# Neighbour lists of a four-layer graph network: the lists of 18 of 26 tiles made inside the first layer, in four parts, instead of all lists ahead of it

## The chip, the cores and the metric

The kernel runs on one core of a Trainium2 chip. A core has a matrix engine (TensorE, PE in the profile), a vector engine (VectorE, DVE), a scalar engine (ScalarE, ACT), a general engine (GpSimd, POOL) and an engine that mainly starts transfers (SyncE, SP). Each runs its own queue of instructions in order; they wait for one another through semaphores. The metric is the device time of one execution in microseconds (us). The kernel before takes 2420.07 us, the median of three runs (2419.6 to 2422.44).

## The reference

There are 3327 nodes with 512 features each, and a 0/1 matrix `adj` of 3327 x 3327 with about 0.5% ones, symmetric and with a full diagonal. Four graph-attention layers follow one another, each of this kind:

```python
h = jnp.maximum(_layernorm(x, axis=-1), 0.0)
h = (h @ W).reshape(n, heads, d)
e = leaky_relu(e_src[:, None, :] + e_dst[None, :, :])   # e_src, e_dst: h times two vectors
e = jnp.where(mask[:, :, None], e, -jnp.inf)            # mask: the neighbours in adj
alpha = jax.nn.softmax(e, axis=1)
x = x + jnp.einsum('ijh,jhd->ihd', alpha, h)
```

The layers have 8, 4, 1 and 8 heads; some of them end with an ELU. The sorted tiles are dimensioned for at most 11 to 36 neighbours, so a layer needs, for every node, the rows of its few neighbours and not the whole matrix.

## The kernel before, in words

**The first stage** (functions within `tile_gat_stack`) reads `adj` in 26 tiles of 128 rows. For each row it finds the columns of the neighbours, up to 40 of them, and keeps them in `L` (128 x 26 x 40, line 633). It also projects the features of the first layer and writes them as rows into the table `tabx` in device memory. Nodes are then sorted by their number of neighbours: `rank` (line 742) is a node's place in that order, `hi` the tile of 128 places it falls into and `lo` its place within the tile (lines 747 to 750). Tile 0 holds the nodes with most neighbours (36 at most), tile 25 those with fewest (11 at most); `CAPS` has these bounds.

**The lists.** The loop at line 764 carries each node's neighbours from the node's first place to its sorted place. It is a product with one-hot matrices: `low[:, t, :]` (line 781) is 1 where a column is the `lo` of the node in that row; the right side (`every`, line 774, or `spare`, line 785) has the neighbour numbers of tile t's nodes in the columns of the tile named by `hi`, and zeros elsewhere; 26 matmuls (line 789) add up one part. There are two parts: part a, the tiles 18 to 25 (120 columns), and part b, the tiles 1 to 17 at 25 columns each and tile 0 at 36 (461 columns). ScalarE copies each result into `idx` and, doubled, `twice` (lines 790 and 791). Part b's right sides go through two buffers in turn, so VectorE and TensorE take turns. After this comes the branch of line 793, on a flag `bad`; the normal case goes to `tile_gat_lists`.

**The layers** (`tile_gat_lists`). A layer goes through the sorted tiles from 25 down to 0. A tile's neighbours are taken in groups: in the first layer 3 gathers first, one of them of a double row that also holds the node's own `x`, then 4 at a time. One group is one step of a loop written out by hand; its pieces are put into each engine's queue in the order in which the loop emits them. For a step s:

- `fetch` (line 865): GpSimd starts one gather for each neighbour (line 838, `g<-tabx`), each moving 128 rows named by a column of `idx` or `twice`. The buffers `g` exist five times (`LOOK`), so the gathers of a group need the products of the group five before it to be done.
- `scored` (line 882) of step s + 1: VectorE adds and bends the scores (`z`, lines 900 and 902), ScalarE takes the exponential (line 903). In the first layer ScalarE also replaces the list entries by ranks (line 906) and keeps the node's own row in `x` (line 908).
- `group` (line 912) of step s: VectorE multiplies each neighbour's row by its weight (line 931, `m<-g` or `bank<-g`), and TensorE adds the rows up in a bank (line 936). As scores of step s + 1 stand ahead of the products of step s in VectorE's queue, the products of a group wait for the rows of the next group too.
- When a tile's last group is done, its `divisors`, `means`, `added`, `root` and so on follow over the next steps, then four transposes (line 454) and the projection for the next layer (line 472), whose rows SyncE writes to the table `tab`.

The first layer has more in its steps. `Weights` of the next layer are loaded as soon as the object is made, ahead of the layer (lines 393 and 395), and `fold` (lines 408 and 410) multiplies them by the attention vectors: three folds after each of the steps 0, 1 and 2 (eight in all). For the third layer, which treats its nine largest tiles densely, nine `Mask` steps, at places 18, 28, ..., gather whole rows of `adj` into `low` (1.7 MB each), ScalarE makes them bf16 (line 1050), TensorE transposes them, and ScalarE puts the pieces into a part of `L` (line 1062), from which SyncE writes them to `found`, four pieces for each mask. `low` and `L` are free by then, as the lists are done.

Of the kernel before, what the change touches and what calls it, by code (L numbers as in the profile page):

```python
# [38 lines left out]
ROUND = 1.5 * 2.0 ** 23  # L39

# [340 lines left out]
class Weights:  # L381
# [3 lines left out]
    def __init__(self, nc, pool, work, l, ws, avs):  # L385
        F = ws[l].shape[0]
        HF, KC = F // 2, F // P
        self.l, self.H, self.D = l, HEADS[l], F // HEADS[l]
        self.nc, self.work, self.HF = nc, work, HF
        self.w = pool.tile([P, KC, 2, HF + 8], F32, name="w")  # L390
        self.av = pool.tile([P, 2, F], F32, name="av", bufs=1)
        for s in range(2):
            nc.sync.dma_start(self.w[:, :, s, :HF],
                              ws[l][:, s * HF:(s + 1) * HF].rearrange("(k p) n -> p k n", p=P))
            nc.sync.dma_start(self.av[:, s, :], bass.AP(tensor=avs[l].tensor, offset=avs[l].offset + s * F,
                                                        ap=[[0, P], [1, F]]))
        if self.H < 8:
            nc.vector.memset(self.w[:, :, :, HF + self.H:], 0.0)
        self.left = [(s, k) for s in range(2) for k in range(KC)]

# [98 lines left out]
class Slots:  # L499
# [16 lines left out]
    def __init__(self, pool, NT):  # L516
        self.parts = [self.Part(pool, "a", [(18, NT)]), self.Part(pool, "b", [(1, 18), (0, 1)])]
# [10 lines left out]
def tile_gat_stack(ctx: ExitStack, tc: tile.TileContext, x, adj, adjT, ws, avs, out):  # L528
# [32 lines left out]
    spare = late.tile([P, 2, slots.parts[1].columns], F32, name="spare")  # L561


    with ExitStack() as c1:
# [39 lines left out]
        def constants():  # L604
            nc.gpsimd.memset(ones, 1.0)
            nc.gpsimd.memset(upper, 1.0)
            nc.gpsimd.affine_select(upper, upper, [[1, P]], OP.is_gt, 0.0, base=0, channel_multiplier=-1)
            nc.gpsimd.memset(sofar, 0.0)
            nc.gpsimd.memset(base[:, 0:1], 0.0)
            nc.scalar.activation(ahead, counting(P, 1, 0, 0), AF.Copy)  # L610
            nc.scalar.activation(bins, counting(BINS, -1, KMAX, 0), AF.Copy)
            nc.scalar.activation(one, ones[:, 0:1], AF.Copy)

# [77 lines left out]
        with tc.manual_schedule(engines={mybir.EngineType.Pool, mybir.EngineType.DVE}):  # L691
            for t in range(NT):
# [6 lines left out]
                if t == 1:  # L699
                    W = Weights(nc, wpool, work, 0, ws, avs)  # L700
# [12 lines left out]
                if t == 0:  # L713
                    constants()
# [20 lines left out]
        with tc.manual_schedule(engines={mybir.EngineType.Pool, mybir.EngineType.PE,  # L735
# [10 lines left out]
            hi = small.tile([P, NT], F32, name="hi", bufs=1)  # L746
# [6 lines left out]

            junk = small.tile([P, BINS], F32, name="junk")
# [3 lines left out]
            nc.tensor.matmul(pn[0:1, :3], ones[:, 0:1], wrong, start=True, stop=True)  # L758
            worst = small.tile([1, 1], F32, name="worst", bufs=1)
            nc.vector.tensor_reduce(worst, pn[0:1, :3], AX.X, OP.max)  # L760
            nc.vector.tensor_copy(bad, worst)


            for i, part_ in enumerate(slots.parts):
                t0, t1 = min(b[0] for b in part_.blocks), max(b[1] for b in part_.blocks)
                high = fixed[:, 304:512] if i == 0 else ps_k.tile([P, BANK], F32, name="high")
                high = high[:, :NT * (t1 - t0)].rearrange("p (t h) -> p t h", h=t1 - t0)
                nc.vector.tensor_tensor(high, ahead[:, t0:t1].unsqueeze(1).to_broadcast([P, NT, t1 - t0]),
                                        hi.unsqueeze(2).to_broadcast([P, NT, t1 - t0]), OP.is_equal)
                n = part_.columns  # L770
                if i == 0:
                    (_, _, k, _), = part_.blocks
                    every = once.tile([P, NT, n], F32, name="every")
                    nc.vector.tensor_tensor(every.rearrange("p t (h k) -> p t h k", k=k),
                                            L[:, :, :k].unsqueeze(2).to_broadcast([P, NT, t1 - t0, k]),
                                            high.unsqueeze(3).to_broadcast([P, NT, t1 - t0, k]), OP.mult)
                pi = ps_i.tile([P, BANK], F32, name="pi")
                for t in range(NT):
                    if i == 0:
                        rhs = every[:, t, :]  # L780
                        nc.vector.tensor_scalar(low[:, t, :], ahead, lo[:, t:t + 1], None, OP.is_equal)
                    else:
                        rhs = spare[:, t % 2, :]
                        for b0, b1, k, c in part_.blocks:
                            nc.vector.tensor_tensor(
                                rhs[:, c:c + (b1 - b0) * k].rearrange("p (t k) -> p t k", k=k),
                                L[:, t, :k].unsqueeze(1).to_broadcast([P, b1 - b0, k]),
                                high[:, t, b0 - t0:b1 - t0].unsqueeze(2).to_broadcast([P, b1 - b0, k]), OP.mult)
                    nc.tensor.matmul(pi[:, :n], low[:, t, :], rhs, start=(t == 0), stop=(t == NT - 1))
                nc.scalar.activation(part_.idx, pi[:, :n], AF.Copy)  # L790
                nc.scalar.activation(part_.twice, pi[:, :n], AF.Copy, scale=2.0)
# [3 lines left out]
    with cond.Else():  # L795
        tile_gat_lists(tc, x, adj, ws, avs, out, ident, half, slots, L, low, spare, tabx, tabs)
# [3 lines left out]
def tile_gat_lists(ctx: ExitStack, tc: tile.TileContext, x, adj, ws, avs, out, ident, half, slots, L, low, spare, tabx, tabs):  # L800
# [24 lines left out]
    xs = [xpool.tile([P, F], F32, name=f"x{t}") for t in range(NT)]  # L825
# [8 lines left out]
    nc.vector.memset(zero, 0.0)  # L834
    L, low, spare = [t.rearrange("p a b -> p (a b)") for t in (L, low, spare)]
# [13 lines left out]
    class Tile:  # L849
# [29 lines left out]
        def scored(self, i):  # L879
# [20 lines left out]
            nc.vector.tensor_tensor(z, g[:, :n, ROW - 8:ROW - 8 + H],  # L900
# [133 lines left out]

    class Mask:
# [5 lines left out]
        def fetch(self):  # L1041
            self.a = low.bitcast(I32)
            gather(self.a, adj, slots(self.t, 0))
# [15 lines left out]
        def keep(self, c0, c1):  # L1059
            def piece():  # L1060
                u = L.bitcast(U8)[:, c0 * P:c1 * P]
                nc.scalar.activation(u, self.pt[:, :(c1 - c0) * P], AF.Copy)
                n = P // 4
                nc.sync.dma_start(found.rearrange("(j p) c -> p j c", p=P)[:, c0:c1, self.t * n:(self.t + 1) * n],
                                  u.bitcast(I32).rearrange("p (j c) -> p j c", c=n))
# [299 lines left out]
    for l in range(NL):  # L1365
# [3 lines left out]
        with ExitStack() as c2:  # L1369
# [30 lines left out]
            else:  # L1400
                scores = itertools.cycle([pools["p"].tile([P, BANK], F32, name="pw") for _ in range(2)])
# [4 lines left out]
            if l == 0:  # L1406
                for t in range(ND):
                    steps.insert(18 + 10 * t, (Mask(t), 0))
                steps[-8:] = [s for i, step in enumerate(steps[-8:]) for s in (step, (Ranked(i), 0))]
                steps += [(Ranked(j), 0) for j in range(8, NT)]  # L1410
            if whole:
# [5 lines left out]
            for s in range(-1, at_end):  # L1417
# [16 lines left out]
                if s == 16 and l + 2 < NL:  # L1434
                    following = Weights(nc, wpool, work, l + 2, ws, avs)
                if l == 0 and s in (0, 1, 2):
                    for _ in range(3):
                        W.fold()
# [46 lines left out]
```

## Time and profile before

| what | value |
| --- | --- |
| median of three runs | 2420.07 us |
| profiled execution, its own time | 2419.54 us |
| its span in the profile | 2417.8 us |
| PE, DVE, ACT, POOL busy | 2068.3, 1885.1, 936.3, 1739.5 us |
| sorting done (`lo`), from the span's start | 257.35 us |
| part a of the lists made (`low` of line 781, matmuls, copies) | 257 to 270.8 us |
| part b made | 268.7 to 295.7 us |
| first gather of the first layer issued | 271.24 us |
| first product of the first layer | 300.76 us |
| first layer's gathers end | about 900 us |

How to read it: "busy" is the time in which an engine executed instructions; the time it spends in starting transfers is shown as idle with the remark "issue". A line of a timeline gives start and duration in us, engine, source line, operation, output and inputs, how many were merged, and in brackets the idle time just before and what ended it. A group has its busy time, the mean of one instruction in ns, and its idle time. In the table of windows, each engine has its busy time and, in brackets, its number of instructions; "PEclk" is the clock granted to TensorE as a share of full speed.

### The profile page before, as it was taken

To read this page: it belongs to the slowest core of one execution; us is meant where nothing else is said; L and a number is where in the kernel's file an instruction comes from. 1 tells how busy PE (TensorE), PEld (TensorE's weight loads), DVE (VectorE), ACT (ScalarE), POOL (GpSimd) and SP (SyncE) were. 2 spreads that over 40 slices of the span, in tenths; PEclk is the share of its full clock that TensorE was granted. 3 is DMA by queue.
4 is the path that set the end of the run, shared out by engine and by line. 5 is a ranking of instruction groups with operands and counts; after the bars stand their busy time and mean duration, and the time that the engine had idled before them with its cause. 6 is when DMAs were issued, how large, how long until landed. Compare 5 with 4: busy or idle time off the path is not lost.

```text
span 2417.8 us, 27489 instructions
## 1 busy us (share of the span) xinstructions
PE 2068.3 (86%) x7298; PEld 1197.0 (50%) x7298; DVE 1885.1 (78%) x4857; ACT 936.3 (39%) x2528; POOL 1739.5 (72%) x1717
## 2 busy tenths in 40 slices
PE   2778779888988885898999987899898699999997
PEld 1656334444444432454455544456565465556653
DVE  7988788877777763888888884888878578888886
ACT  5777113434331111433333332544443444344430
POOL 7899267777777776766677772778778467777775
PEclk9988899999999997999999998999999899999999
DMA  5887569999998788887888884889887578888885
GB/s 227 316 299 248 153 192 299 276 299 282 286 283 237 234 231 241 242 245 235 234 261 255 256 237 141 270 262 283 268 248 240 161 226 256 250 243 246 252 241 176
DMA packets 260732, 594.23 MB, mean 246 GB/s; under 512 B 103699, under 2 KB 121107, under 8 KB 256214
## 3 DMA queue, kind: packets, MB, share of 16 engines
q0 software_dynamic: 124368, 432.13, 59.5%
q1 hardware_dynamic: 132454, 153.45, 19.6%
q10 hardware_dynamic: 3744, 6.82, 0.8%
q8 instruction: 59, 0.97, 0.2%
q14 instruction: 107, 0.88, 0.1%
HBM read 542.60 MB, written 49.65 MB: 245 GB/s over the span
## 4 chain that ended last, share of the span: by engine, by line
DVE 31%; DMA 17%; PE 16%; issue 13%; POOL 12%; ACT 9%; DVEq 0%; SPq 0%; ACTq 0%; POOLq 0%
DVE m L931 13%; POOL g L838 8%; DMA g<-tab,idxb 6%; PE bank L936 5%; DMA g<-tabx,twiceb 4%; PE pv L472 4%; PE whole L1173 3%; POOL key L698 3%; DVE bank L924 3%; ACT r L1280 2%; DMA g<-tab,idxa 2%; DVE room L1296 2%; DVE z L902 2%; ACT pw L903 2%; DVE z L900 1%
## 5 line engine op out<-in xcount | busy, mean ns | idle before, releaser
L936 PE MATMUL bank<-m,ident 128*128 128x512 f32 x2414 | 1128.0, 613 | 144.8 <-DVE m L931 144.3
L838 POOL DMA_INDIRECT g<-tab,idxb x712 | 683.1, 959 | 236.0 <-issue 162.0
L931 DVE TENSOR_TENSOR m<-g,pw 128x512 f32<-128x512 f32 x1207 | 752.2, 682 | 100.2 <-ACT pw L903 99.6
L936 PEld LDWEIGHTS bank<-m,ident 128*128 128x128 f32 x2414 | 448.7, 194 | 689.2 <-issue 314.6
L472 PE MATMUL pv<-w,hT 128*128 128x264 f32 x1664 | 431.5, 413 | 67.8 <-ACT hT L461 44.5
L903 ACT ACTIVATE pw<-z 128x32 f32<-128x32 f32 (+4 forms) x356 | 68.2, 191 | 988.9 <-DVE z L902 988.9
L472 PEld LDWEIGHTS pv<-w,hT 128*128 128x128 f32 x1664 | 331.7, 203 | 166.8 <-ACT hT L461 50.8
L838 POOL DMA_INDIRECT g<-tab,idxa x297 | 286.3, 964 | 165.0 <-issue 110.6
L838 POOL DMA_INDIRECT g<-tabx,twiceb x342 | 324.0, 947 | 106.0 <-issue 79.5
L1173 PE MATMUL whole<-ve,em 128*128 128x512 f32 x468 | 217.8, 612 | 16.3 <-DVE em L1152 11.2
L698 POOL TENSOR_TENSOR key<-a,keys 128x3328 int32<-128x3328 int32 (+1 forms) x29 | 189.3, 6530 | 16.3 <-DVE cand L707 11.8
L924 DVE SCALAR_TENSOR_TENSOR bank<-g,L,bank 128x512 f32<-128x512 f32 x243 | 183.3, 754 | 6.8
L900 DVE TENSOR_TENSOR z<-g,pw 128x32 f32<-128x32 f32 (+4 forms) x356 | 62.6, 176 | 152.1 <-DMA g<-tabx,twiceb 64.7
L1314 PEld LDWEIGHTS whole<-L,room 128*128 128x128 f32 x1248 | 147.5, 190 | 24.9 <-issue 19.1
L838 POOL DMA_INDIRECT g<-tabx,twicea x99 | 94.9, 959 | 78.5 <-issue 38.1
L1314 PE MATMUL whole<-L,room 128*128 128x130 f32 x1248 | 147.8, 274 | 0.0
L707 DVE MAX8 cand<-key 128x8 f32<-128x208 int32 x416 | 144.0, 364 | 0.1
L1173 PEld LDWEIGHTS whole<-ve,em 128*128 128x128 f32 x468 | 88.1, 196 | 109.2 <-issue 87.2
L1280 ACT ACTIVATE r<-low,L 128x384 f32<-128x384 f32 x208 | 121.2, 583 | 5.1
L454 PE MATMUL pt<-ident,xn 128*128 128x128 f32 x416 | 65.4, 281 | 35.4 <-ACT hT L461 13.6
L454 PEld LDWEIGHTS pt<-ident,xn 128*128 128x128 f32 x416 | 52.5, 145 | 68.6 <-issue 28.3
L931 DVE TENSOR_TENSOR bank<-g,pw 128x512 f32<-128x512 f32 x74 | 51.5, 696 | 37.4 <-ACT pw L903 36.6
(180 smaller groups left out, 2192.6 us busy)
## 6 DMA issues: line engine op xcount, KB each, us to landing
a<-in_adj SPq DMA_DIRECT2D x25, 1664.0 KB
tab<-v SPq DMA_DIRECT2D x78, 264.0 KB
ve<-tab SPq DMA_DIRECT2D x78, 264.0 KB
g<-tab SPq DMA_DIRECT2D x65, 264.0 KB
tabx<-vx SPq DMA_DIRECT2D x26, 528.0 KB
g<-tab,idxb POOLq DMA_INDIRECT x712, 4.0
low<-tab SPq DMA_DIRECT2D x52, 132.0 KB
spare<-tab SPq DMA_DIRECT2D x52, 132.0 KB
```

What stands on the lines that cost most here:

```text
L454: nc.tensor.transpose(pt[:, k, :], xn[:, k * P:(k + 1) * P], ident)
L472: nc.tensor.matmul(pv[:, s, :HF + 8], hT[:, k, :], W.w[:, k, s, :], start=(k == 0), stop=(k == KC - 1))
L698: nc.gpsimd.tensor_tensor(key[:, c:c + quarter], a[:, c:c + quarter], keys[:, c:c + quarter], OP.mult)
L707: nc.vector.max(cand[:, g * 8:(g + 1) * 8], key[:, g * SEG:(g + 1) * SEG])
L838: nc.gpsimd.indirect_dma_start(out=out_, out_offset=None, in_=table, in_offset=bass.IndirectOffsetOnAxis(ap=which, axis=0))
L903: nc.scalar.activation(self.wt[:, k0:k0 + n, :H], z, AF.Exp)
L924: nc.vector.scalar_tensor_tensor(acc, v, w, acc, OP.mult, OP.add)
L931: nc.vector.tensor_tensor(out_.rearrange("p (s h d) -> p s h d", s=2, d=D), v.rearrange("p s (h d) -> p s h d", d=D), wt[:, k0 + q, :H].re ...
L936: nc.tensor.matmul(self.po, ident, m[:, q, :], start=False, stop=(k0 + q == K - 1), skip_group_check=True)
L1173: nc.tensor.matmul(tl.po.rearrange("p (s m) -> p s m", s=2), e[:, q * P:(q + 1) * P], v.rearrange("p (s m) -> p s m", s=2)[:, :, :F // 2], ...
L1280: nc.scalar.activation(self.r[:, h, :], self.a[:, g, :], AF.Relu, bias=-1.0, scale=self.b[:, j, g:g + 1])
L1314: nc.tensor.matmul(dst, e[:, h, q * P:(q + 1) * P], mov, start=False, stop=(j == NT - 1), skip_group_check=True)
```

## The change

The list `slots` has five parts instead of two: a with the tiles 18 to 25 as before (120 columns), b with 14 to 17 (68 columns), c with 9 to 13 (95), d with 4 to 8 (105) and e with 1 to 3 and 0 (111). Only part a is made ahead of the branch, together with nine columns `own` for the nodes' own places in tiles 0 to 8. The one-hots `low` of the last ten tiles are made by GpSimd from a copy of the column numbers in SBUF, the right side `every` is made in two pieces (tiles 0 to 4, then 5 to 25), and the doubled copy comes before the plain one.

The parts b to e are made within the first layer by the new class `Lists`: at a step VectorE makes the right side of one tile in one instruction (two for part e) into one of eight short buffers in `spare`, and TensorE multiplies it at the next step. The 26 tiles of a part are spread over the steps before its first gather: part b over steps 1 to 26, c over 27 to 47, d over 48 to 76, e from 76 on. ScalarE's two copies follow at steps 28, 49, 77 and 107.

Since `low` and `L` stay in use, the masks go to `xall[:, :NP]`, the storage of tiles 0 to 6 of `x`, and their transposed pieces all go through one 896-byte place in `xall`; masks stand at steps 14, 23, ... instead of 18, 28, .... The score banks of the first layer share one PSUM bank, since a bank is needed for the lists. The next layer's weights are loaded when the first scores are computed (a wait of SyncE on that VectorE instruction), and folded one at a time, after steps 2 to 9. Tiles of `x` become parts of one tile `xall`.

```diff
+OURS = 16
...
+        self.given = ws[l], avs[l]
...
+    def load(self, tc=None, behind=None):
+        (w, av), nc, HF = self.given, self.nc, self.HF
...
+                if behind is not None:
+                    tc.add_manual_dep(made.ins, behind.name, ...)
...
-        self.parts = [self.Part(pool, "a", [(18, NT)]), self.Part(pool, "b", [(1, 18), (0, 1)])]
+        self.parts = [self.Part(pool, name, blocks) for name, blocks in
+                      [("a", [(18, NT)]), ("b", [(14, 18)]), ("c", [(9, 14)]), ("d", [(4, 9)]), ("e", [(1, 4), (0, 1)])]]
+        self.own = pool.tile([P, ND], I32, name="idxown")
...
+            nc.vector.tensor_copy(nth, columns[:, :NT])
...
+            nc.vector.tensor_tensor(every[:, :, n:], nth[:, :ND].unsqueeze(1).to_broadcast([P, NT, ND]),
+                                    hi.unsqueeze(2).to_broadcast([P, NT, ND]), OP.is_equal)
+            nc.gpsimd.tensor_tensor(every[:, :, n:], every[:, :, n:],
+                                    L[:, :, 0:1].to_broadcast([P, NT, ND]), OP.mult)
+            for t in range(OURS, NT):
+                nc.gpsimd.tensor_scalar(low[:, t, :], columns, lo[:, t:t + 1], None, OP.is_equal)
...
-            for i, part_ in enumerate(slots.parts):
...
+            sides(0, 5)
...
+            chosen(0, 5)
+            sides(5, NT)
+            chosen(5, NT)
+            nc.scalar.activation(part_.twice, pi[:, :n], AF.Copy, scale=2.0)
+            nc.scalar.activation(part_.idx, pi[:, :n], AF.Copy)
+            nc.scalar.activation(slots.own, pi[:, n:n + ND], AF.Copy)
...
-            nc.vector.tensor_tensor(z, g[:, :n, ROW - 8:ROW - 8 + H],
+            self.known = nc.vector.tensor_tensor(z, g[:, :n, ROW - 8:ROW - 8 + H],
...
+    class Lists:
+        def __init__(self, i, bank):
+            self.part = slots.parts[i]
+            self.pi = bank[:, :self.part.columns]
+        def side(self, t):
+            return spare[:, t % 8 * 115:t % 8 * 115 + self.part.columns]
+        def sides(self, t):
+            for b0, b1, k, c in self.part.blocks:
+                nc.vector.scalar_tensor_tensor(
+                    self.side(t)[:, c:c + (b1 - b0) * k].rearrange("p (h k) -> p h k", k=k),
+                    nth[:, b0:b1].unsqueeze(2).to_broadcast([P, b1 - b0, k]), hi[:, t:t + 1],
+                    by_tile[0][:, t, :k].unsqueeze(1).to_broadcast([P, b1 - b0, k]), OP.is_equal, OP.mult)
+        def chosen(self, t):
+            nc.tensor.matmul(self.pi, by_tile[1][:, t, :], self.side(t),
+                             start=(t == 0), stop=(t == NT - 1))
+        def kept(self):
+            nc.scalar.activation(self.part.idx, self.pi, AF.Copy)
+            nc.scalar.activation(self.part.twice, self.pi, AF.Copy, scale=2.0)
+        def place(self, s0, steps):
+            last = max(b[1] for b in self.part.blocks) - 1
+            due = next(s for s, (tl, i) in enumerate(steps) if isinstance(tl, Tile) and tl.t == last) - LOOK - 1
+            for t in range(NT):
+                s = s0 + t * (due - 1 - s0) // NT
+                later(s, "last", lambda t=t: self.sides(t))
+                later(s + 1, "last", lambda t=t: self.chosen(t))
+            later(due, "last", self.kept)
+            return due - 1
...
-            self.a = low.bitcast(I32)
-            gather(self.a, adj, slots(self.t, 0))
+            self.a = xall[:, :NP].bitcast(I32)
+            gather(self.a, adj, slots.own[:, self.t:self.t + 1])
...
-                u = L.bitcast(U8)[:, c0 * P:c1 * P]
+                u = xall[:, NP:7 * F].bitcast(U8)[:, :(c1 - c0) * P]
...
-                scores = itertools.cycle([pools["p"].tile([P, BANK], F32, name="pw") for _ in range(2)])
+                banks = [pools["p"].tile([P, BANK], F32, name="pw") for _ in range(2)]
+                scores = iter([banks[0][:, i % 2 * 256:(i % 2 + 1) * 256] for i in range(NT - 1)] + banks[1:])
...
-                    steps.insert(18 + 10 * t, (Mask(t), 0))
+                    steps.insert(14 + 9 * t, (Mask(t), 0))
...
+                s = 1
+                for i in range(1, len(slots.parts)):
+                    s = Lists(i, banks[1]).place(s, steps)
...
-                if l == 0 and s in (0, 1, 2):
-                    for _ in range(3):
-                        W.fold()
+                if l == 0 and s == 0:
+                    W.load(tc, steps[0][0].known.ins)
+                if l == 0 and 2 <= s <= 9:
+                    W.fold()
```

## The prediction

> **What bounds the kernel now.** I read the stretch around the lists: first GpSimd's timeline, since the first layer's gathers all go through its queue.
>
> ```profile
> 271.24 1.19 POOL L838 DMA_INDIRECT g<-tabx,twicea  x1 [29.15 <-DMA av<-in_a]
> 272.73 0.95 POOL L838 DMA_INDIRECT g<-tabx,twicea  x1 [0.30 <-issue]
> ...
> 303.39 0.94 POOL L838 DMA_INDIRECT g<-tabx,twicea  x1 [9.72 <-issue]
> ...
> 310.79 0.94 POOL L838 DMA_INDIRECT g<-tabx,twicea  x1 [2.58 <-DVE prod L408]
> 317.90 1.24 POOL L838 DMA_INDIRECT g<-tabx,twicea  x1 [6.17 <-issue]
> ...
> 324.04 0.94 POOL L838 DMA_INDIRECT g<-tabx,twicea  x1 [2.20 <-ACT pw L903]
> ```
>
> A gather takes 0.95 us and 0.30 us of issue, so one goes every 1.25 us. The first starts once part a is copied; 18 go into the five buffers, and then GpSimd stops. Over 0.30 us each, the four gaps come to 9.42 + 2.28 + 5.87 + 1.90 = 19.5 us. The table of windows tells that none follow:
>
> ```profile
> core 0: us, PE busy (x) PEld busy (x) DVE busy (x) ACT busy (x) POOL busy (x), PEclk, DMA share, GB/s
> 300.00:324.00 24.00, 16.51 (x26) 6.00 (x25) 21.23 (x43) 2.29 (x12) 8.18 (x8) 0.77 0.35 90
> 350.00:400.00 50.00, 47.15 (x164) 26.05 (x163) 39.98 (x114) 17.62 (x45) 37.81 (x40) 1.00 0.92 286
> 450.00:500.00 50.00, 43.06 (x142) 22.79 (x141) 40.04 (x105) 15.69 (x39) 37.81 (x40) 0.97 0.94 306
> 500.00:550.00 50.00, 45.40 (x159) 24.82 (x158) 39.77 (x116) 21.73 (x46) 36.60 (x39) 0.97 0.90 285
> 800.00:850.00 50.00, 41.99 (x113) 20.23 (x112) 34.06 (x85) 8.40 (x30) 37.81 (x41) 1.00 0.78 229
> ```
>
> Forty gathers at 1.25 us fill 50 us: GpSimd's issue bounds the layer from 324 to about 897 us, with one gap (2.13 us at 513). So the layer's end moves with the sum of GpSimd's gaps. Why the gaps are there, VectorE's timeline shows:
>
> ```profile
> 292.11 1.48 DVE L785 TENSOR_TENSOR spare<-L,high 128x425 f32<-128x425 f32 x4 [0.36 <-PE pi L789]
> 298.35 0.06 DVE L833 MEMSET one<- 128x1 f32 x1 [4.77 <-issue]
> ...
> 300.76 0.70 DVE L931 TENSOR_TENSOR bank<-g,pw 128x512 f32<-128x512 f32 x1 [0.81 <-PE bank L1395]
> ```
>
> Part b keeps VectorE until 293.6, the branch takes 4.77, and only the products from 300.76 on free a buffer. Then six folds of 1.44 us (lines 408 and 410) go between the first groups.
>
> How near VectorE is to being the bound later I read as slack: the start of a group's first gather less the end of the products five groups earlier. For the second group of tile 22 that is 340.29 - 339.07 = 1.2 us, for that of tile 21 1.7; from tile 20 to 17 it is 4 to 9, in tiles 15 to 13 (472 to 527 us) 0.7 to 4, behind that mostly 4 to 9. About 0.75 is what shows when GpSimd does wait.
>
> **The change, part by part.**
>
> *Part b taken out.* VectorE loses 24 us (269.3 to 293.6). GpSimd already worked beside it, so the path loses only the gaps: 19.5 us at most, and the 1.8 at 513 if that goes too.
>
> *First gather.* Before it: sorting done at 257.35, part a's work, TensorE done at 270.36, the copies, 271.24. New on VectorE: `nth` and `own`'s 234 columns (0.17 and 0.39, by the 208-column row of 0.36). From 257.4 I count 0.6 for these, 0.85 for `junk`, `wrong` and `high`, 0.7 for 600 columns of `every` (3.40 for 3120), 0.35 for `worst` and `bad`, 1.3 for five one-hots at 0.26: 261. Then 2.75 for 2520 columns and 2.9 for eleven one-hots: 266.7, against 268.7 now. GpSimd's ten one-hots: 0.45 each, from its 7.27 for 3328 elements and 1.01 for 384 (at least 0.29, the 128-column select; at most 1.01). It ends at about 263 (269 at most), and its branch, 2.9 (ScalarE's gap) to 4.8 us, is then hidden (273.5 at worst). TensorE decides: its 26 matmuls are now 129 columns wide, and its clock is the point.
>
> ```profile
> 264.00:266.00 2.00, 2.00 (x11) 2.00 (x11) 2.00 (x9) 0.00 (x0) 0.00 (x0) 0.50 0.62 168
> 266.00:268.00 2.00, 2.00 (x18) 2.00 (x18) 2.00 (x9) 0.00 (x0) 0.00 (x0) 0.89 0.91 232
> 268.00:270.00 2.00, 2.00 (x20) 2.00 (x20) 1.97 (x7) 0.00 (x0) 0.00 (x0) 1.00 0.83 238
> ```
>
> The same window table: at half clock a matmul of 120 columns takes 0.4 us, at full clock 0.2, and the clock rose some 4 us after TensorE began at 262.3. In the new order it does five until 262.2, waits until 264.2 for the rest of `every`, and does 21. If the clock rises at 266.7 these end at 270, if never at 273.2. With `twice` first (0.3 saved) I take 0 for the first gather, between 1.2 earlier and 3 later.
> The Trainium skill, "TensorE: Matmul & The Clock Gate", Part 1, says that full clock comes after about 3.4 us of sustained activity and is lost after an idle window of that length. By it the pause restarts the count, the clock rises at 267.6 and the matmuls end at 270.4: an estimate that makes the sum 0.4 worse.
>
> *The layer's beginning.* ScalarE (2.85 us of branch after 270.9) and TensorE (clearing the banks took 2.0 for the first) are ready by 278. The products of group 0 stand behind the scores of group 1, whose last gather is issued at 271.2 + 6 x 1.25 = 278.7. A landing takes this long (the rows of `g`, 271 to 420 us):
>
> ```profile
> DMA to landing us min/median/max: 3.6/4.5/8.1
> ```
>
> So the first product comes at 283.7, 17 us earlier, while the gather that started at 324.04 could go 19.5 us earlier. From there I wrote out VectorE's queue group by group: 0.63 a product, 0.75 for scores with ScalarE's answer, 0.2 a right side, 0.6 for `divisors`, 2.0 for `root`, 1.6 for `means` and `added`, and 1.44 for each of the eight folds, now after steps 2 to 9. The products of groups 7, 10 and 11 end at 321.5, 335.7 and 341.0; GpSimd wants their buffers at 320.65, 335.3 and 339.4, so it waits 0.9 + 0.4 + 1.6 = 2.9 us.
> Two things come on top. The weights, 1.5 MB, went beside nothing (374 GB/s at their best around 265 us); now they are issued at some 280 and share the engines with groups 2 to 4: 0 to 4 us of delay, I take 1.6. SyncE waits for the first scores; behind that stands only the row writes of tile 25, some 40 us later. And masks now stand at steps 14 and 23, where the slack is least. In the layer VectorE waits 48.0 us for ScalarE's `pw` in 94 places; 0.31 each is the plain answer, so 19 us belong to nine masks, 2.1 each, of which 1.25 is paid by the mask's own place in GpSimd's queue. The pieces of a mask now wait for the write of the one before: 0.92 for the copy, 0.36 issue, 3.9 to land (3.2 to 6.4) is 5.2 us against a step of 5.0, ScalarE's exponentials queueing behind. I take 1.5 for both. Together 6 us, between 2 and 10.
>
> *Lists inside.* VectorE gets 130 instructions: by the 36- and 425-column rows and their spacing 0.17, 0.20, 0.21 and 0.33 us a tile for b, c, d and e, x 26 = 23.7 us. Its cover is the wait for rows:
>
> ```profile
> DVE z L900 <- DMA g<-tabx,twiceb: 59.0, 32, 6.0
> ```
>
> That is its longest wait between 320 and 900 us; but 45 of the 59 fall behind 580, and c's sides (5.2 us) meet the tiles 18 to 14. With the slack read there I take 2 us of new gaps, between 0 and 4. TensorE gets 104 matmuls of about 0.2 us (line 1314: 130 columns in 0.22), 21 us against 79 idle ones between 320 and 920; ScalarE eight copies of 0.27, with 71% of it idle. Each list is copied six steps before its first gather, and GpSimd is about two ahead of VectorE, so it waits for no list; if a list were late, the gap would be that of tiles 15 to 13 again.
>
> *The rest.* From the second layer on all engines' orders are the same. SyncE gets no more transfers.
>
> **The sum**, against the profiled execution's own 2419.54 (0.5 below the median): -19.5 + 0 + 6 + 2 = -11.5, so 2408.0, and 2408.5 by the median. With the ends: -19.5 - 1.2 + 2 + 0, and 1.8 for the gap at 513, is -20.5; -19.5 + 3 + 10 + 4 is -2.5: 2399.5 to 2417.5.
>
> **Rivals.**
> *Nearly all is kept* (2399 to 2403): VectorE's added work fits into its waits. For: its busy share is 80%. Against: slack of 1.2 to 1.7 at tiles 22 and 21, where folds and sides now go. 0.15.
> *Early groups and masks give back more* (2413.5 to 2418): the ring of one piece and the weights beside the gathers at their dear ends. For: a landing of up to 8.1 in these rows. 0.15.
> *VectorE becomes the bound of the whole layer* and it is slower: its products begin 17 us earlier, and all 23.7 us of right sides lie on its path: 2419.5 + 6.7 = 2426. It decides from 17 us of exposed sides on. Against: the waits for rows behind 580. 0.06.
> *The beginning doesn't move*: the first scores, a list or the branch wait for something new, for instance a late GpSimd or cold TensorE, and the gaps return elsewhere: 2416 to 2424. 0.06.
>
> **How the numbers follow.** Likeliest, 2403 to 2413.5: 0.58. The range for 8 in 10 takes the ends of the unknown costs: 2399 to 2418. A difference under 0.2%, 4.8 us, can't be told from none. Faster than that: 0.58 + 0.15 and half of the next, 0.81; same: the other half and most of the last, 0.12; slower 0.07.
>
> **What would show it.** GpSimd's gathers from 270 to 274 on, without a gap over 3 us until 400; the first product at 283 to 285; VectorE's `prod` one a step; no `pi` matmuls behind 271; VectorE's wait for rows down from 59 to about 40. Wrong would be: gaps in GpSimd's queue named after ScalarE or `pm` at each mask, or a total in them over 15 us between 295 and 600.

## The result and the profile after

The changed kernel takes 2435.68 us (median of five runs, 2431.35 to 2436.77) against 2422.0 us of the kernel before beside it: ratio 1.0053, interval 1.0041 to 1.0064. It is 13.7 us slower; I had forecast 11.5 us faster. The span of its profiled execution is 2435.0 us.

GpSimd's timeline of the changed kernel has both halves of it. The columns are start, duration, engine, line, operation, output and inputs, number, and the idle time before with what ended it:

```profile
271.33 1.23 POOL L864 DMA_INDIRECT g<-tabx,twicea  x1 [7.17 <-ACT idxown L814]
...
294.70 0.95 POOL L864 DMA_INDIRECT g<-tabx,twicea  x1 [0.87 <-DVE z L928]
...
301.65 0.94 POOL L864 DMA_INDIRECT g<-tabx,twicea  x1 [1.00 <-issue]
...
306.41 0.95 POOL L864 DMA_INDIRECT g<-tabx,twicea  x1 [1.30 <-issue]
...
327.97 0.95 POOL L864 DMA_INDIRECT g<-tabx,twicea  x1 [4.80 <-issue]
...
348.36 0.95 POOL L864 DMA_INDIRECT g<-tabx,twicea  x1 [2.52 <-issue]
...
868.41 0.95 POOL L864 DMA_INDIRECT g<-tabx,twicee  x1 [0.30 <-issue]
```

The first gather starts where it did (271.24 before), and the gather that had started at 324.04, behind the four gaps, starts at 306.41. So 17.7 us were gained, as the prediction's first term has it. But gaps go on: of those over 0.6 us, less 0.30 each, some 34 us lie between 295 and 605 us. The last line is the first gather of tile 0's third group; it stands 597.1 us behind the first gather. In the kernel before the same gather stands 581.9 us behind the first one (271.24):

```profile
853.18 0.95 POOL L838 DMA_INDIRECT g<-tabx,twiceb  x1 [0.30 <-issue]
```

**I use this distance from the first gather as the measure of the layer below**, because it leaves out how long the sorting took, which differs between executions (first gathers at 269.6 to 275.2 us). It is read from one execution of each kernel; in the thirteen kernels compared here its change differs from the timed one by 0.2 to 3.5 us, so a difference of 2 or 3 us in it is not certain by itself. It is 15.1 us longer now. Put tile by tile, GpSimd is ahead of the kernel before by 17.7 us in tile 23, 8.3 in tile 21 and 1.0 at the start of tile 16, and behind it by 5.1 at tile 13 and 16.6 at tile 9. From there on it keeps its 15 us.

The windows of the changed kernel (busy time and number for each engine, clock, share of the DMA engines, GB/s):

```profile
core 0: us, PE busy (x) PEld busy (x) DVE busy (x) ACT busy (x) POOL busy (x), PEclk, DMA share, GB/s
300.00:324.00 24.00, 17.06 (x48) 8.13 (x46) 20.82 (x56) 3.23 (x12) 15.80 (x17) 0.98 0.73 208
350.00:400.00 50.00, 47.36 (x188) 28.32 (x187) 38.19 (x117) 19.86 (x43) 36.35 (x39) 1.00 0.89 279
450.00:500.00 50.00, 43.72 (x175) 25.25 (x173) 40.44 (x113) 17.78 (x41) 33.56 (x36) 1.00 0.88 264
500.00:550.00 50.00, 41.48 (x142) 23.98 (x143) 36.65 (x105) 15.74 (x39) 31.97 (x34) 0.87 0.87 274
800.00:850.00 50.00, 42.52 (x115) 20.85 (x114) 36.29 (x95) 9.44 (x32) 37.80 (x41) 0.97 0.81 238
```

GpSimd is at 37.80 only at the end; between 450 and 550 it is at 32 to 34, so it waits for buffers, and VectorE frees those. Yet VectorE is at 36.7 to 40.4 of 50 there, where it was at 39.8 to 40.0. It isn't full; it waits. For what, the waits from 306 to 912 us tell (engine, line, waited for: total us, times, longest), VectorE first, then ScalarE:

```profile
DVE m L957 <- ACT pw L929: 55.1, 87, 3.7
DVE z L926 <- DMA g<-tabx,twicee: 30.3, 18, 3.8
DVE bank L957 <- ACT pw L929: 17.8, 23, 4.3
DVE ve L1016 <- ACT waste L1011: 8.8, 8, 1.6
DVE z L926 <- DMA g<-tabx,twiced: 6.5, 6, 2.2
DVE spare L1073 <- PE pw L1079: 4.8, 2, 2.8
...
ACT xall L1124 <- DMA found<-xall: 63.4, 18, 5.8
```

VectorE's wait for the exponentials (`pw`) before its products `m` has grown by 25 us. In the kernel before, 324 to 900 us, it was:

```profile
DVE m L931 <- ACT pw L903: 30.2, 71, 2.8
```

And ScalarE waits 63.4 us for something that it never waited for before: the write of a mask's piece to `found`, which has to leave the one 896-byte place before the next piece may enter.

### The profile page after: what moved, and what is told of

It reads as the page before. It is cut to its first block, busy times and chain, and to the rows that moved or that the text cites. A ratio compares the mean times of both kernels' runs of the same rounds, so it can differ in the third digit from the quotient of the medians.

```text
span 2435.0 us, 27930 instructions
## 1 busy us (share of the span) xinstructions
PE 2076.4 (85%) x7454; PEld 1224.7 (50%) x7454; DVE 1889.5 (78%) x4927; ACT 940.2 (39%) x2535; POOL 1747.7 (72%) x1728
## 4 chain that ended last, share of the span: by engine, by line
DVE 25%; PE 15%; DMA 15%; issue 10%; ACT 7%; POOL 6%; DVEq 0%; SPq 0%; ACTq 0%; POOLq 0%
DVE m L957 12%; POOL g L864 6%; PE whole L1235 5%; PE bank L962 4%; DMA g<-tab,idxd 3%; PE pv L484 3%; DVE bank L950 2%; DMA g<-tab,idxa 2%; ACT r L1342 2%; DVE room L1358 2%; ACT pw L929 1%; DVE z L928 1%; DMA g<-tabx,twicee 1%; DMA g<-tab,idxe 1%; DMA found<-xall 1%
## 5 line engine op out<-in xcount | busy, mean ns | idle before, releaser
L962 PE MATMUL bank<-m,ident 128*128 128x512 f32 x2414 | 1143.5, 619 | 165.4 <-DVE m L957 164.6
L864 POOL DMA_INDIRECT g<-tab,idxc x252 | 244.6, 971 | 92.2 <-issue 55.9
L864 POOL DMA_INDIRECT g<-tab,idxd x192 | 182.1, 948 | 58.5 <-issue 44.5
L864 POOL DMA_INDIRECT g<-tab,idxb x180 | 172.9, 961 | 59.2 <-issue 41.0
L864 POOL DMA_INDIRECT g<-tabx,twicee x102 | 96.7, 948 | 31.1 <-issue 26.2
L864 POOL DMA_INDIRECT g<-tabx,twiced x96 | 91.0, 948 | 29.4 <-issue 22.7
```

Of the source, the lines that this page charges most:

```text
L864: nc.gpsimd.indirect_dma_start(out=out_, out_offset=None, in_=table, in_offset=bass.IndirectOffsetOnAxis(ap=which, axis=0))
L962: nc.tensor.matmul(self.po, ident, m[:, q, :], start=False, stop=(k0 + q == K - 1), skip_group_check=True)
```

## The experiments

Each kernel was timed beside the kernel before, and its ratio is against that. The kernel before took 2420.8 to 2423.8 us on these occasions, so kernels timed at different times are compared by their ratios.

**First question: masks, sides or weights?** Theory M blames the one place for a mask's pieces, theory V the 130 right sides on VectorE, theory W the weights beside the first gathers.

The first kernel gives the four pieces four places:

```diff
-                u = xall[:, NP:7 * F].bitcast(U8)[:, :(c1 - c0) * P]
+                at = NP, 7 * F, 7 * F + 256, 8 * F
+                if self.t == ND - 1:
+                    at = NP, 0, 256, 512
+                at = at[c0 // 7]
+                u = xall[:, at:at + 256].bitcast(U8)[:, :(c1 - c0) * P]
```

> The changed kernel, with the four pieces of a mask in four places of xall in place of one. Theory M: ScalarE waits 63.4 us in 18 places for the mask's own row writes, the exponentials queue behind these waits, and VectorE's products behind the exponentials; without the waits most of the 33 us that the layer gives back between tiles 23 and 9 stays, 2408 to 2420 us. Theory V: the 130 right sides on VectorE fill the time that it used to wait, whatever ScalarE does: 2428 to 2436.

Measured: 2420.25 us, ratio 0.9986 (0.9977 to 0.9995); the layer's distance is 582.1, 15.0 less than in the changed kernel. That is a hair above theory M's range and far below theory V's: the one place takes the whole loss against the kernel before, but not the gain that was forecast on top of it. How 63 us of waiting on ScalarE become 15 us is seen in ScalarE's timeline of the changed kernel, tile 12:

```profile
565.38 0.92 ACT L1124 ACTIVATE xall<-pm 128x896 uint8<-128x896 bf16 x1 [2.43 <-PE pm L1118]
566.20 0.20 ACT L929 ACTIVATE pw<-z 128x32 f32<-128x32 f32 x1
...
569.62 0.92 ACT L1124 ACTIVATE xall<-pm 128x896 uint8<-128x896 bf16 x1 [3.10 <-DMA found<-xall]
570.43 0.20 ACT L929 ACTIVATE pw<-z 128x32 f32<-128x32 f32 x1
...
574.42 0.92 ACT L1124 ACTIVATE xall<-pm 128x896 uint8<-128x896 bf16 x1 [3.19 <-DMA found<-xall]
575.24 0.20 ACT L929 ACTIVATE pw<-z 128x32 f32<-128x32 f32 x1
...
581.35 0.70 ACT L1124 ACTIVATE xall<-pm 128x640 uint8<-128x640 bf16 x1 [5.79 <-DMA found<-xall]
581.95 0.18 ACT L929 ACTIVATE pw<-z 128x16 f32<-128x16 f32 x1
```

and of the same steps with four places:

```profile
553.97 0.92 ACT L1128 ACTIVATE xall<-pm 128x896 uint8<-128x896 bf16 x1
...
555.32 0.20 ACT L929 ACTIVATE pw<-z 128x32 f32<-128x32 f32 x1 [0.43 <-DVE z L928]
...
557.85 0.20 ACT L929 ACTIVATE pw<-z 128x32 f32<-128x32 f32 x1 [0.60 <-DVE z L928]
...
561.89 0.20 ACT L929 ACTIVATE pw<-z 128x32 f32<-128x32 f32 x1 [1.47 <-DVE z L928]
...
565.23 0.19 ACT L929 ACTIVATE pw<-z 128x16 f32<-128x16 f32 x1 [1.25 <-DVE z L928]
```

With one place the exponential has no wait of its own; it stands directly behind the copy, and the copy behind the write. From the first to the fourth exponential it takes 15.75 us, with four places 9.91. GpSimd, at four gathers of 1.25 us, has a pace of 15 us for three steps. So VectorE, which would go faster than GpSimd here and make up what it had lost on the mask, is held at GpSimd's pace or below.

The second kernel puts the one place into the kernel before:

```diff
-                u = L.bitcast(U8)[:, c0 * P:c1 * P]
+                u = L.bitcast(U8)[:, :(c1 - c0) * P]
```

> The kernel before, with the four pieces of a mask in one place in place of four, nothing else. Theory M: ScalarE waits some 50 to 60 us for the writes here too; GpSimd is 4 to 9 us ahead of need in most of the layer and takes a part of it, 2425 to 2437. Theory V: the waits are hidden as before, 2420 to 2424.

Measured: 2425.31 us, ratio 1.0012 (1.0003 to 1.0021), the layer 5.3 us longer. ScalarE waits as long and as often as in the changed kernel, and VectorE's wait for the exponentials grows by 25 us here too; from the table of waits, 324 to 900 us:

```profile
ACT L L1062 <- DMA found<-L: 63.3, 18, 5.8
...
DVE m L931 <- ACT pw L903: 55.3, 70, 4.8
...
DVE z L900 <- DMA g<-tabx,twiceb: 37.1, 21, 6.2
```

But the last line, VectorE's longest wait for rows, was 59.0 us in the kernel before. So here most of the 25 us came out of time in which VectorE would have waited for rows anyway.

The same 63 us thus cost 3.4 us (timed) or 5.3 (in the trace) here and 15 there. Theory M has the cause, but its price isn't a property of the wait.

The third kernel loads the weights ahead of the layer again:

```diff
-    following = Weights(nc, wpool, work, 1, ws, avs)
+    following = Weights(nc, wpool, work, 1, ws, avs).load()
...
-                if l == 0 and s == 0:
-                    W.load(tc, steps[0][0].known.ins)
```

> The changed kernel, with the weights of the second layer loaded ahead of the layer, not behind the first scores. Theory W, that the 1.5 MB beside the gathers of groups 1 to 4 (whose first products came 14 us after their last issue, not 9) started a delay that is never made up: 2422 to 2430. Theories M and V: the beginning is 3 to 6 us better, and the wait for the banks behind it takes this back, 2430 to 2436.

Measured: 2430.52 us, ratio 1.0032 (1.0022 to 1.0041), the layer 6.4 us shorter than in the changed kernel. That is at the edge between the two expectations, and tells that the weights have a price of their own (timed, some 5 us). VectorE's timeline of the changed kernel shows the place:

```profile
284.32 1.28 DVE L957 TENSOR_TENSOR m<-g,pw 128x512 f32<-128x512 f32 x2
294.12 0.19 DVE L926 TENSOR_TENSOR z<-g,pw 128x32 f32<-128x32 f32 x1 [8.52 <-DMA g<-tabx,twicea]
```

The last of the rows that it waits for here was asked for at 284.1 us (the group's gathers start at 280.36, one each 1.25 us). So the rows came 13.8 us after the group's first gather was issued and 10.0 after its last; the "14 us after their last issue" of the expectation is counted from the first. With the weights loaded early the same wait is 3.05 us.

The fourth kernel is the kernel before with the 130 right sides added by the changed kernel's rule for the steps, into `spare`, where nobody reads them; its lists are made as before:

```diff
+                        def side(t=t, blocks=blocks):
+                            c = t % 8 * 115
+                            for b0, b1 in blocks:
+                                k = CAPS[b0]
+                                nc.vector.scalar_tensor_tensor(
+                                    spare[:, c:c + (b1 - b0) * k].rearrange("p (h k) -> p h k", k=k),
+                                    ident[:, b0:b1].unsqueeze(2).to_broadcast([P, b1 - b0, k]), one,
+                                    ident[:, :k].unsqueeze(1).to_broadcast([P, b1 - b0, k]), OP.is_equal, OP.mult)
+                                c += (b1 - b0) * k
+                        later(s0 + t * (due - 1 - s0) // NT, "last", side)
```

> The kernel before, with 130 right sides more on VectorE inside the layer, at the steps where the change makes them and of its sizes, into storage that nobody reads. Theory V: VectorE has no room for them, 2432 to 2445. Theory M: they lie in its waits for rows, 2420 to 2427.

Measured: 2424.33 us, ratio 1.0011 (1.0000 to 1.0022), the layer 0.5 us longer. Alone, the sides are nearly free: VectorE is busy 27.2 us longer (1912.3 for 1885.1), of which 2.4 us show in the time (0 to 5.3 by the interval). TensorE's 104 matmuls, ScalarE's eight copies and the shared score bank, which the lists also bring, are not in this kernel, and no run has them alone.

**Second question: what else is given back, and does it add up?**

> The changed kernel with a mask's four pieces in four places and the second layer's weights loaded ahead of the layer. Theory M+W (two separate prices, the masks' 15 us and the weights' 5): they add, 2413 to 2417. Rival S (one shortage of VectorE, which either relief takes away only once): 2418 to 2421.

Its edit is the first and the third together. Measured: 2417.49 us, ratio 0.9977 (0.9965 to 0.9989); the layer is 576.8, another 5.3 us shorter. Timed, it lies at the border of the two expectations, only some 2 us from the first kernel by the ratios, with intervals that overlap; that the prices add is said by the trace alone.

The next kernel also moves the eight folds:

```diff
+            while l == 0 and W.left:
+                W.fold()
             at_end = len(steps) + 30
...
-                if l == 0 and 2 <= s <= 9:
-                    W.fold()
```

> The kernel of the run above, with all eight folds of the weights ahead of the layer's first step, where VectorE waits 13 us for the first rows. Theory F (the folds at steps 2 to 9, beside the sides of the second part, are what is left of the loss in tiles 24 to 21, 9 us in the run with four pieces): 4 to 9 us faster than the run above, 2406 to 2412. Rival: what is left there is the sides and the exponentials' round trip, and the folds only go elsewhere, within 2 us of the run above.

Measured: 2409.49 us, ratio 0.9949 (0.9930 to 0.9967), the layer 568.3, another 8.6 us shorter: theory F, at its full price. The folds fill a hole on VectorE and delay hardly anything: the first product comes 12.7 us after the first gather, in the run above 12.6. VectorE's timeline:

```profile
268.50 0.09 DVE L395 MEMSET w<- 128x32 f32 x1
273.79 0.69 DVE L420 TENSOR_TENSOR prod<-w,av 128x512 f32<-128x512 f32 x1 [5.20 <-issue]
...
284.64 0.69 DVE L422 TENSOR_REDUCE w<-prod 128x4 f32<-128x512 f32 x1
285.25 0.16 DVE L918 COPY pw<-g 128x8 f32<-128x8 f32 x1
...
286.75 0.19 DVE L926 TENSOR_TENSOR z<-g,pw 128x32 f32<-128x32 f32 x1 [0.91 <-DMA g<-tabx,twicea]
```

Sixteen instructions from 273.8 to 285.3, and then VectorE still waits 0.9 us for rows. In the changed kernel the time from 266 to 279 was empty.

Two variations of this kernel followed. In one the masks stand four steps later, and the last two masks, not the last one alone, use the second set of places, as tile 8 is in use by then:

```diff
-                    steps.insert(14 + 9 * t, (Mask(t), 0))
+                    steps.insert(18 + 9 * t, (Mask(t), 0))
```

> The run with the folds ahead, with the masks at steps 18 + 9t, not 14 + 9t. The prediction's reason (the masks stand where the slack is least): 1 to 3 us faster than the folds ahead alone. If the masks cost by their storage alone: within 1 us of it.

Measured: 2415.77 us, ratio 0.9971 (0.9958 to 0.9983); the layer is 7.7 us longer. Both expectations missed: later is worse. The trace shows where: 5.7 of the 7.7 us are lost within tile 17, where the second list has just ended and the third begins.

```profile
400.37 2.96 ACT L1112 ACTIVATE m<-xall 128x3328 bf16<-128x3328 int32 x1
403.34 0.21 ACT L1084 ACTIVATE twiceb<-pw 128x68 int32<-128x68 f32 x1
403.61 1.17 PE L1079 MATMUL pw<-spare,low 128*128 128x95 f32 x4 [7.30 <-ACT twiceb L1084]
411.38 0.92 ACT L1128 ACTIVATE xall<-pm 128x896 uint8<-128x896 bf16 x1 [7.10 <-PE pm L1118]
415.05 0.94 POOL L864 DMA_INDIRECT g<-tabx,twiceb  x1 [4.09 <-issue]
```

All lists are added up in one bank, so TensorE's first matmul of the third list has to wait for ScalarE's copies of the second. With the masks at these steps a mask's 2.96 us on ScalarE stands ahead of these copies. TensorE waits 7.30 us; its clock, which was 1.00 up to 398 us, is at 0.50 when it goes on, and its projection (line 484, 16 matmuls) takes 5.95 us for 3.78 in the run with the folds ahead. ScalarE then waits for TensorE's transposes of the mask, with an exponential behind it. So the run is slower mostly by a collision of a mask with the change of lists, and it can't tell whether the slack at the masks' steps matters.

In the other, `OURS` is 26, so that VectorE makes all one-hots:

> The run with the folds ahead, with the ten one-hots of the first part on VectorE, not GpSimd: 2.6 us more on VectorE before TensorE's last products of the list. If VectorE sets the first gather: 2 to 3 us slower than the folds ahead alone; if TensorE does, as the prediction has it: 0 to 1 us slower.

Measured: 2409.32 us, ratio 0.9953 (0.9936 to 0.9971). The first gather stands ahead of the layer's distance; counted from the end of the sorting (`lo`) it comes after 15.6 us, and after 15.4 in the run with the folds ahead. GpSimd's ten one-hots gain nothing that can be measured.

**Third question: why has the same wait two prices?** Theory C says that it depends on how far VectorE is ahead.

> The run with the folds ahead, with the mask's four pieces in one place again, as in the changed kernel. If the waits for the mask's writes cost 15 us wherever they stand: 2423 to 2427 us. Theory C (their price depends on how far VectorE is ahead of GpSimd's need; 3 us in the kernel before, 15 where folds, sides and late rows had used that up): 4 to 10 us slower than with the folds ahead and four places, 2413 to 2420.

Its edit takes back the four places from the run with the folds ahead. Measured: 2422.19 us, ratio 1.0007 (0.9995 to 1.0019), the layer 11.9 us longer. That is far nearer to the full price: with folds and weights out of the way the one place costs 12 us (timed 14), not 15. So theory C as I had put it falls; folds and late rows are not what made the wait dear. What is left that the kernel before doesn't have is the lists, with their sides on VectorE, and earlier steps for the masks. The next kernel doubles the sides.

> The run with the folds ahead, with every right side written twice, 23.7 us more on VectorE. Theory V: the sides are on the path in tiles 24 to 9, each us costs some 0.6, 12 to 16 us slower than the folds ahead alone. Theory C: they lie in VectorE's waits once nothing else takes these, as in the kernel before (2.4 us for all of them): 2 to 7 us slower.

The edit is `self.part.blocks * 2` in the loop of `sides`. Measured: 2433.08 us, ratio 1.0053 (1.0036 to 1.0070), the layer 21.9 us longer (25 by the ratios), so both ranges are missed. The work is more than the 23.7 us estimated: VectorE is busy 34.3 us longer than in the run with the folds ahead (1926.0 for 1891.7). Behind a side of the second part the next instruction starts after 0.20 us, but its twin, written to the same place, after 0.33. So the second set cost some 0.64 of its length, near theory V's 0.6, while the first, 27.2 us in the kernel before, cost 0.5 us of the layer. This fits a cover that is used up, such as VectorE's waits for rows. In the part of the layer where the loss arose, 300 to 600 us, the tables of waits show it. The kernel before:

```profile
DVE z L900 <- DMA g<-tabx,twiceb: 9.5, 6, 3.3
DVE z L900 <- DMA g<-tabx,twicea: 3.5, 4, 2.0
```

with one place for the pieces:

```profile
DVE z L900 <- DMA g<-tabx,twicea: 1.7, 2, 0.9
...
DVE z L900 <- DMA g<-tabx,twiceb: 0.6, 1, 0.6
```

with the sides:

```profile
DVE z L900 <- DMA g<-tabx,twiceb: 3.0, 2, 2.5
```

Each alone took some 10 of the same 13.0 us. The next kernel puts both into the kernel before:

> The kernel before with both, the 130 right sides on VectorE (alone: GpSimd's last gather of the layer 0.5 us later in the trace) and a mask's pieces in one place (alone: 5.3 us later). Theory C2 (each alone was paid by the same cover, VectorE's 13.0 us of waiting for rows between 300 and 600 us, of which the one left 3.0 and the other 2.3): together they find it once, the last gather 14 to 22 us later, 2434 to 2444 us. If their prices add: 6 us later, 2425 to 2430.

Measured: 2433.4 us, ratio 1.0057 (1.0043 to 1.0070); the layer is 9.4 us longer, and no wait for rows is left between 300 and 600 us. Timed, 0.57% stands against 0.12% and 0.11% alone, 12.6 us against 5.8 by adding (the trace: 9.4 against 5.8). That is well above the sum, but the 2433.4 us lie just under theory C2's range, and the trace's 9.4 well under its 14 to 22: the cover is shared, and it is larger than the waits for rows alone, by what was not measured.

The place of the waits counts as well. Between 300 and 600 us lie 35.4 of ScalarE's 63.3 us of waiting in the kernel before with one place, and 35.9 with the sides added, but 49.1 in the run with the folds ahead and one place, as its masks stand at earlier steps. Behind 600 us the waits cost little: where tile 10 starts, at 580 to 590 us, 4.9 of the 5.3 us are lost in the first of these kernels and 10.5 of the 11.9 in the last. For each us of waiting before 600, the one place costs 5.3 / 35.4 = 0.15 us in the kernel before, (9.4 - 0.5) / 35.9 = 0.25 beside the sides, and 11.9 / 49.1 = 0.24 in the run with the folds ahead. By this estimate the sides and the masks' earlier steps together account for the 12 us. No run moves the masks of the kernel before alone, so their share is not shown.

**A version that beats both.** In the run with the folds ahead VectorE still waited for TensorE before a right side, 400 to 530 us:

```profile
DVE spare L1073 <- PE pw L1079: 4.9, 2, 3.0
```

Every list began at the first of the eight storages again, which held the last but one side of the list before. The next kernel counts them on:

```diff
-            return spare[:, t % 8 * 115:t % 8 * 115 + self.part.columns]
+            q = (NT * self.i + t) % 8
+            return spare[:, q * 115:q * 115 + self.part.columns]
```

> The run with the folds ahead, with the eight storages of right sides counted on from one list to the next, so that a list's first side does not go where the last list's last but one lies. It had VectorE wait 4.9 us in 2 places for TensorE's products of the list before (400 to 530 us, tiles 17 to 13). If that wait is on the path: 2 to 4 us faster than the folds ahead alone; if the exponentials behind a mask's copies set these tiles: within 1 us.

Measured: 2406.58 us, ratio 0.9943 (0.9926 to 0.9960). That line is gone from its waits, and the layer is another 2.9 us shorter in the trace; by the ratios the difference to the run with the folds ahead is 1.5 us, within the intervals. GpSimd's timeline, first gather and the one in tile 0:

```profile
273.57 1.23 POOL L864 DMA_INDIRECT g<-tabx,twicea  x1 [7.71 <-ACT idxown L814]
...
838.94 0.94 POOL L864 DMA_INDIRECT g<-tabx,twicee  x1 [0.30 <-issue]
```

565.4 us between them, 16.6 less than in the kernel before. It has all of the change, and four things mended.

## Why the prediction was wrong

The distances make a ledger from this version back to the changed kernel, each price as it came when the things were mended one after another:

| step of the layer, first gather to tile 0 | us | distance to the kernel before |
| --- | --- | --- |
| all four mended | 565.4 | -16.6 |
| sides begin at the first storage in every list | +2.9 | -13.7 |
| folds at steps 2 to 9 | +8.6 | -5.1 |
| weights beside the gathers | +5.3 | +0.1 |
| one place for a mask's pieces | +15.0 | +15.1 |

- **The gaps removed, -19.5: right.** GpSimd is 17.7 us ahead at the gather that ended the last gap before, and 18.6 to 20.0 in the runs with the weights early. The 1.8 us at 513 did not go; the gaps there grew.
- **The first gather, 0: right within its bounds, and partly by luck.** 271.33 for 271.24, but the sorting ended 0.3 us earlier in that execution. From the end of the sorting it is 14.3 us for 13.9, and over the profiles 14.3 to 15.4 (median 14.8; the nine kernels with GpSimd's one-hots) for 13.4 to 14.9 (median 13.9; the four with the old order): some 1 us later. TensorE does decide. Its matmuls ended at 270.12, where I had 270. GpSimd's one-hots took 0.58 us each (5.84 for ten), not 0.45, beside TensorE's work. What varies is TensorE's clock. In the changed kernel it rose from 0.50 to 1.00 at 266.9 us, 3.4 us after TensorE had begun again at 263.53, but in the other kernels with this order (the one with all one-hots on VectorE among them) 3.7 to 6.2 us after that, which is 7.6 to 10.1 after its first matmul. In the old order, without a pause, it rose 3.1 to 6.1 us after the first matmul. So the pause of 1.4 us did start the wait anew, as the prediction's estimate by the skill supposed, but the wait has no fixed length. The Trainium skill, "TensorE: Matmul & The Clock Gate", Part 1, has some 3.4 us of sustained activity for it, watched in a window that runs freely; the 3.4 us of the changed kernel are the shortest that this order showed.
- **The layer's beginning, +6: the step that failed.** It had three terms. *Buffers late by VectorE's queue, 2.9:* the folds, which make it, measured 8.6. The places were right: in the run with four places and early weights GpSimd's gaps stand at groups 12, 15 and 16, as forecast, but with 2.8 + 0.7 + 2.2 = 5.7 us for my 0.9 + 0.4 + 1.6; the rest came in tiles 17 and 16, where the lead lost here was missing (gaps of 2.84 and 1.40 us there, with the folds ahead 1.18 and none). *The weights, 1.6:* measured 5.3 to 6.4 in the traces (timed, 2 to 5). I took a moderate value out of 0 to 4, and that range was too short: by the median landing of 4.5 us the rows of the third group were due at 288.6, and VectorE got them at 294.1. *The masks and the one place, 1.5:* measured 15.0 (11.9 where the rest was mended). The mechanism was named ("5.2 us against a step of 5.0", exponentials queueing behind); the size was off tenfold. The 5.0 us is GpSimd's step. What counts is the step of the engine that has to catch up: 2.5 to 4.0 us between exponentials with four places, above. With such steps VectorE can make up the 3 us that ScalarE is away for each mask (line 1112, 2.96 us); writes that take 3.3 to 7.3 us from a copy's end to its release take that from it. This is my reading of the two timelines of tile 12.
- **Lists inside, +2: right alone, wrong in company.** 0.5 to 2.4 us is what the sides cost in the kernel before, though they keep VectorE 27.2 us and not 23.7. The cover was also smaller than I read: 53.5 of the 59.0 us of waits for rows fall behind 580 us, not 45. I used the waits for rows as their cover, and in the same sum the slack of tiles 24 to 21 as cover for folds and masks, without asking whether it was the same cover. It was, in part: the kernel before with both costs 9.4 us of the layer (12.6 timed) where the two alone add up to 5.8. The term that no part of the sum had is 2.9 us in the trace, a wait of a side for the list before.
- **The rivals.** "Early groups and masks give back more" named the right causes and ended at 2418 at most; together they gave back 8.6 + 5.3 + 15.0 = 28.9 us. "VectorE becomes the bound of the whole layer" gave the right side, 2426, with a wrong reason: it isn't the whole layer, since from tile 8 on VectorE has its lead again, and not the sides alone. The loss of 33 us arose within tiles 23 to 9.
- **What was to show it.** First product at 283.72 (283 to 285), one `prod` a step, no `pi` behind 271, VectorE's wait for rows at 36.8 where about 40 was said: these came as announced, and did not tell the outcome. "No gap over 3 us until 400" failed: the gap at 327.97 has 4.80 us. And the sign of the wrong case came: a total over 15 us of gaps between 295 and 600. Only their name was different, as the wait passes through VectorE: the remark at most of the gaps is "issue", not ScalarE's.

What remains unexplained is some 3 us between the 19.4 us gained and the 16.6 kept in the best version. They lie mostly in two gaps of GpSimd, 2.12 us in tile 17 and 2.35 in tile 13; the kernel before has one of 2.13 in tile 13. What makes them was not tested.

## What to carry to other kernels

When a storage gets fewer places, compare the time of the write that empties it not with the average step, but with the shortest step of the engine that must catch up behind it, and look at what stands behind the waiting copy in the same queue. A cover (an engine's idle time, the lead given by buffers) is used up by what it pays for: list all that is to hide in it, by stage, and subtract, before any of them is called free. Work that has to be done early goes into the hole that the change itself opens; here the hole of 13 us before the first rows took all the folds and gave 8.6 us.

## What the runs showed that was not expected

The same wait of ScalarE, 63.3 and 63.4 us in 18 places each, cost 5.3 us of the layer in one kernel and 15.0 in the other, and 130 instructions of 27.2 us cost 0.5 us once, while their twins of 34.3 us cost 21.9 in a kernel that already had them. And masks four steps later in the same list of steps cost 7.7 us of the layer, more than the weights beside the gathers, mostly because one of them met the change of lists.
